# Slice-norm transfers issued by ScalarE and GpSimd in place of SyncE, and a new order of all instructions

## The chip, the cores and the metric

The kernel runs on one core of a Trainium2 chip. Five engines work side by side: TensorE (PE) multiplies matrices, VectorE (DVE) and ScalarE (ACT) do element-wise work, GpSimd (POOL) does small odds and ends, and SyncE (SP) issues the transfers. Each engine takes its own instructions strictly in the order in which the program lists them, and waits on semaphores for the others. An instruction that waits holds everything behind it on its engine. The metric is device time in microseconds; the median of three executions before the change is 2547.61 us (2545.12 to 2547.99).

## What is computed

The input `x` is 32 batches of 512 rows with 256 features, and `adj` is a 512x512 mask. One layer is computed:

```python
x = x + gnn(layernorm(x), adj)     # two graph attention layers
x = x + ffn(layernorm(x))          # attention over slices

# gnn
out = relu(x @ mlp1_w + mlp1_b)                     # 256 -> 512
out = elu(gat(out, None, W_fc, a_fc)) + out         # every row attends to every row
out = relu(out @ mlp2_w + mlp2_b)                   # 512 -> 256
out = relu(elu(gat(out, adj, W_hand, a_hand)) + out)

# ffn: 8 heads of 64, 64 slices
slice_weights = softmax((x_mid @ W_slice + b_slice) / temp)
slice_norm = slice_weights.sum(axis=2)
slice_token = einsum('bhnc,bhng->bhgc', fx_mid, slice_weights) / (slice_norm + 1e-05)
attn = softmax(q @ k.T * SCALE)                     # 64x64 per head, of the tokens
out_x = einsum('bhgc,bhng->bhnc', attn @ v, slice_weights)
return out_x @ W_out + b_out
```

The change concerns how `slice_norm`, a row of 512 sums per batch, travels from the row of a matrix product to the tile that divides the tokens by it.

## The kernel before

The kernel does not issue its operations as it writes them. It builds a list with a recorder: `nc` is a `Recorder`, and each call such as `nc.vector.tensor_tensor(...)` becomes an operation with a batch (`age`) and a stage (`step`). All 32 batches are recorded, batch by batch, as `front` (layer norm, first layer), `middle` (second layer) and `back` (second layer norm and slices). Then `Recorder.order` lays out one order for each engine, and `emit` issues it.

The order comes from list scheduling with a table of costs. `_cost` gives each operation an engine time and a lag; transfers also get a time of moving, during which the modelled transfer queue is taken (`ISSUE`, `BEGIN`, `LAND`, `BEHIND`). `_schedule` then takes, again and again, the operation that can start first, and among those that can start, the one with the lowest key. The keys come from the table `TURNS`, one number per stage, from `PERIOD`, and for the first three and last three batches from the shifts in `HEAD` and `TAIL`. These numbers and the costs decide only which instruction stands where on its engine. On the chip the semaphores decide the times. Up to four batches are in work at once, so that TensorE is given matmuls of one batch while the others do their element-wise work and transfers. In the trace all recorded operations have one line, L289, so groups are told apart by the names of their tiles.

The stages of a batch, with the names that the text below uses:

- `norm1`: layer norm of `xt`. VectorE makes statistics, GpSimd makes `rstd` (two small instructions on 128x4), VectorE makes `xn`.
- `xnT`: the transposed `xn`. In all but the first and last batch, transposes of this size are made in two steps. VectorE flips 32x32 blocks into a stage (`xn_stage`), and SyncE writes the stage to DRAM in four transfers (`scr<-xn_stage`) and reads it back in another order (`xnT<-scr`). The same is done for `u` (to `o1T`), `e` (to `p2T`), `o2` (to `r2`), `w` (to `w_raw`, which ScalarE copies to `wT`) and `xn2` (to `xn2_raw`, which ScalarE copies to `xn2T`).
- `mlp1`, `h`: matmuls of `xnT` with `w1` to `o0T`; then `h` by Strassen's scheme, for which VectorE makes four sums `mix` of blocks of `o0T`.
- `factors`, `p`: a maximum over rows by a transpose of `fm`, a transpose of `sc`, exponentials `acb`, and from them `pT`, the attention matrix of the first layer.
- `pv`, `o1`: 32 matmuls `mm<-h,pT`; the double ELU on VectorE and ScalarE gives `u`, whose transpose is added to `o0T` to make `o1T`.
- `mlp2`, `h2`, `e`, `p2`, `pv2`: the second graph layer, with the matmuls `mm<-o1T,w`, `mm<-wh,o2T` and `mm<-h,p2T`, and a second double ELU, which gives `x1`.
- `norm2`, `w`: the second layer norm, again with `rstd` on GpSimd, gives `xn2` and `xn2T`; the matmuls `mm<-weff,xn2T` and a softmax over each head's 64 slices give `w`, and its flips `w_stage`.
- `sums`, `s1T`: matmuls `mm<-w,xn` sum `xn2` over the rows with the slice weights. The last feature of `xn2` is set to 1, so that the last row of the product holds the norms. ScalarE copies the product to `s1T`.
- `tokens`, `att`, `vo`, `gg`, `out`: small matmuls `mm<-s1T,wfx` make the tokens, VectorE multiplies them by the reciprocal norms (`tok`), a small attention over slices follows (`sc2`, `attT`, `mean`), and 16 matmuls `mm<-gg,wT` give the output, which is added to `x1`.

The norms take this way. Row 127 of `s1T` is one partition with 512 numbers. A transfer spreads it over 128 partitions (`norm`, 128x4); VectorE adds 1e-5 and takes the reciprocal; a second transfer writes it to DRAM (`line`); two more read it back, each to 64 partitions at once (`rn`). Every step waits for the one before. Before the change all four are issued by SyncE, like all other transfers of the batches.

For a batch in the middle SyncE's order before the change runs: `scr<-w_stage` twice, `norm<-s1T`, `scr<-xn_stage` four times, `scr<-w_stage` twice, `xnT<-scr`, `line<-norm`, `w_raw<-scr`, `rn<-line` twice, `scr<-u_stage` four times, `o1T<-scr`, `scr<-xn2_stage` four times, `xn2_raw<-scr`, and then the transfers of `o2`, `out`, `xt`, `e`, `x1` and `p2T`. They belong to different batches.

Of the kernel before, what the change touches and what calls it, by code (L numbers as in the profile page):

```python
# [14 lines left out]
ENGINES = ("tensor", "vector", "scalar", "gpsimd", "sync")  # L15

TURNS = {
    "load": 361.5, "norm1": -64.6, "mlp1": 945.4, "h": 1108, "factors": 1115.3, "p": 1133,
    "pv": 1134.5, "o1": 1135, "mlp2": 1177.7, "h2": 1179.1, "e": 1182.9, "p2": 877, "pv2": 1230.3,
    "norm2": 1235.2, "w": 1273.7, "sums": 1279.8, "s1T": 1239.3, "tokens": 1552, "att": -211,  # L20
    "vo": -118.6, "gg": -952.5, "out": 1227.3,
}
PERIOD, SPARE = 89.08, 0.01

HEAD = (
    (0, -29, 160, 21, 3, -112, -46, -107, 0, -66, -7, -21, -125, -126, 0, 1933, -17, -4, -13, 0,
     9, -230),
    (1280, -6, 24, -107, -16, 42, -95, 0, 52, -257, 0, 10, 10, -15, 6, 922, 199, -1, 61, 0, 14,
     -102),
    (120, 0, 3, 38, 28, 14, 995, 253, 320, -610, 0, 0, 113, -155, 135, -133, -95, 0, -25, 5, -4,  # L30
     -34),
)
TAIL = (
    (279, 0, 0, 0, 0, 17, 0, 0, -104, 0, -939, 31, -14, 0, 1655, 0, 66, 146, 103, 128, 52, 221),
    (-322, 0, -112, 2, -20, 0, -1205, 10, -7, -185, 10, 170, -102, -11, 215, 497, 0, 0, -6, 0,
     76, 63),
    (-107, -134, 0, 190, -47, -204, 0, 86, 13, 5, -3, 0, 4, 11, 273, 574, -226, -28, 78, -10,
     -113, 101),
)


# [4 lines left out]
P = 128  # L46
# [4 lines left out]
class Recorder:  # L51
# [2 lines left out]

    SIGNAL = 0.06
    DRAIN = 0.17
    ISSUE, BEGIN, LAND, BEHIND = 0.45, 2.2, 0.0, 3.6
    SWITCH = 0.17
    KEPT = 1
    AHEAD = 3  # L60
# [66 lines left out]
    def _cost(self, op, out, ins):  # L127


        def words(ap):  # L130
            return ap.size() // ap.ap[0][1]

        n = words(out)
        if op.method == "dma_start":
            side = next(ap for ap in (out, *ins) if ap.space != bass.MemoryType.DRAM)
            kb = out.size() / 256
            if side.ap[0][1] <= P // 4:
                op.moving = 0.3 + max(0.0, 1.08 * (kb / 128 - 1))
            else:
                op.moving = max(1.5 * kb / 512, 4.0 * kb / 1024 - 0.5)  # L140
            return self.ISSUE, 0.0
        if op.engine == "tensor":
            one = max(n / 1200 + 0.002, 0.109)
            if op.mode == (P, P // 2):
                one = max(n / 2400, 0.0275)
            elif op.mode == (P // 2, P // 2):
                one = max(n / 4000, 0.0135)
            return (one if op.method == "transpose" else 2 * one), self.DRAIN
        if op.engine == "scalar":
            pointers = sum(isinstance(op.kwargs.get(k), bass.AP) for k in ("bias", "scale"))  # L150
            return 0.06 + n / 1200 + 0.09 * pointers + 0.19 * ("accum_out" in op.kwargs), 0.12
        if op.engine == "vector":
            n = max([n] + [words(x) for x in ins])
            single = op.method in ("tensor_copy", "tensor_scalar")
            fast = single and all(x.space != bass.MemoryType.PSUM for x in ins)
            if op.method == "reciprocal":
                return 0.05 + n / 145, 0.1
            pointers = sum(words(x) == 1 for x in ins) if n > 1 else 0
            return 0.07 + n / (1920 if fast else 960) + 0.065 * pointers, 0.1
        if n < 16:  # L160
            return (0.1 if op.method == "memset" else 0.3 if op.method == "tensor_scalar" else 1.1), 0.1
        return 0.2 + n / (480 if op.method == "tensor_tensor" else 960), 0.1
# [164 lines left out]
def adj_ffn_kernel(  # L327
# [30 lines left out]
    KD = D // P  # L358
# [5 lines left out]
    NP = INNER // P  # L364
    assert G == C == 64 and HEADS * G == 512 and N == 512 and HID == 512 and D == 256

    nc = Recorder(tc.nc)
# [5 lines left out]
    def ts(i, n=P):  # L373
        return slice(i * n, (i + 1) * n)

    def new(name, shape, bufs=1, tag=None, dtype=F32):
        return sbuf.tile(list(shape), dtype, name=name, tag=tag or name, bufs=bufs)

    def mm_tile(shape):
        return psum.tile(shape, F32, tag="bank", name="mm", bufs=8)  # L380
# [36 lines left out]
    def med(name, shape=(P, 4, 256)):  # L417
        return new(name, shape, bufs=2, tag="med")
# [14 lines left out]
    def load_x(b):  # L433
# [14 lines left out]
        out=ident, in_=ident, compare_op=OP.not_equal, fill=1.0, base=0,  # L448
# [163 lines left out]
    for p in range(NP):  # L612
        pv = mm_tile([P, D])
# [283 lines left out]
    def back(b, x1):  # L897
# [17 lines left out]
        w = new("w", [P, NT, INNER], tag="o0T" if b == B - 1 else None, bufs=1 + (b == B - 1))  # L915
# [34 lines left out]
        s1T = med("s1T", (P, KD, INNER))  # L950
# [14 lines left out]
                )  # L965
        nc.step = "s1T"
        norm = new("norm", [P, NP], bufs=2)
        nc.sync.dma_start(norm, s1T[P - 1 : P, KD - 1, :])
        nc.vector.tensor_scalar(norm, norm, 1e-5, None, op0=OP.add)
        nc.vector.reciprocal(norm, norm)  # L970
        line = dram.tile([NP, 2, G], F32, name="line", tag="line", bufs=2)
        nc.sync.dma_start(line.rearrange("p s (q f) -> (p s q) f", f=NP), norm)
        rn = new("rn", [P, NP, G], tag="mean")
        for s in range(2):
            nc.sync.dma_start(
                rn[ts(s, C)],
                bass.AP(
                    tensor=line.tensor, offset=line.offset + s * G,
                    ap=[[0, C], [2 * G, NP], [1, G]],
                ),  # L980
            )
# [20 lines left out]
        q = new("q", [P, 2, 2, G])  # L1002
# [57 lines left out]
        gg = med("gg")  # L1060
# [33 lines left out]
    for b in range(B):  # L1094
        nc.age = b
        back(b, middle(b, front(b)))
# [57 lines left out]
```

## Time and profile before

| | us |
|---|---|
| median of three executions | 2547.61 |
| lowest and highest | 2545.12, 2547.99 |
| the profiled execution's own time | 2548.94 |
| its span, first to last instruction | 2547.2 |
| VectorE, ScalarE and GpSimd busy | 2041.9, 1095.2, 95.0 |
| transfers, mean share of 16 engines and rate | 49%, 137 GB/s |

The span was taken at a mean granted TensorE clock of 0.995 of full speed. The profile has a page of overviews, and queries for stretches, tiles, waits and an engine's timeline. The slices of the page show the same picture from the first fortieth to the last:

```profile
PE   6999999999999999999999999999999999999998
PEld 5777666666677666666766766666666676667665
DVE  6678778787788887788877888878878878888774
ACT  2544444434435444435344354444443444444442
POOL 0000000000000000000000000000000000000000
```

Each digit is the busy share of a fortieth of the span in tenths. The transfers in question, as the page's list of issues has them, with the issuing queue, count, size and the median time from issue to landing:

```profile
rn<-line SPq DMA_DIRECT2D x64, 64.0 KB, 4.6
...
norm<-s1T SPq DMA_DIRECT2D x32, 2.0 KB, 5.8
line<-norm SPq DMA_DIRECT2D x32, 2.0 KB, 4.3
```

They are small, but each stands in SyncE's queue with everything else.

### The profile page before, as it was taken

The page shows a single profiled execution, that of the slowest core. Times are in us where ns is not written, and L with a number is a line of the kernel's source. Part 1 is how long each engine was busy: PE and PEld are TensorE (multiplying, and loading weights), DVE is VectorE, ACT ScalarE, POOL GpSimd, SP SyncE. Part 2 cuts the span into 40 slices and gives each one's busy share as a digit, 9 for nine tenths or more (in the row PEclk, how much of TensorE's full clock was granted, in tenths as well). Part 3 has the DMA queues.
Part 4 walks back from the last instruction along what each step waited for, and adds up shares of the span by engine and source line. Part 5 has one row for each costly group of instructions (what it writes and reads, how often), then busy time and mean ns, then how long its engine had stood idle before and what let it go on. Part 6 is the DMA issues. An engine that isn't in the chain of part 4 may idle for free.

```text
span 2547.2 us, 34086 instructions
## 1 busy us (share of the span) xinstructions
PE 2493.8 (98%) x11653; PEld 1722.5 (68%) x11653; DVE 2041.9 (80%) x5236; ACT 1095.2 (43%) x2069; POOL 95.0 (4%) x167
## 2 busy tenths in 40 slices
PE   6999999999999999999999999999999999999998
PEld 5777666666677666666766766666666676667665
DVE  6678778787788887788877888878878878888774
ACT  2544444434435444435344354444443444444442
POOL 0000000000000000000000000000000000000000
PEclk8999999999999999999999999999999999999999
DMA  5134455544555544655445554445554455553532
GB/s 161 50 91 111 135 167 154 156 126 119 157 159 159 137 127 124 166 159 151 138 121 143 159 159 135 125 125 168 158 153 133 127 143 161 158 146 106 161 82 63
DMA packets 451139, 348.69 MB, mean 137 GB/s; under 512 B 110228, under 2 KB 375572, under 8 KB 450966
## 3 DMA queue, kind: packets, MB, share of 16 engines
q1 hardware_dynamic: 449382, 345.46, 49.1%
q8 instruction: 93, 1.52, 0.2%
q10 hardware_dynamic: 1584, 1.05, 0.1%
q14 instruction: 80, 0.66, 0.1%
HBM read 186.92 MB, written 159.45 MB: 136 GB/s over the span
## 4 chain that ended last, share of the span: by engine, by line
PE 59%; DVE 20%; DMA 12%; ACT 6%; issue 2%; SPq 1%; POOL 0%; DVEq 0%; ACTq 0%
PE mm L289 57%; DMA scr<-w_stage 4%; DMA w_raw<-scr 3%; DVE e L289 3%; DVE w L289 3%; PE tr L289 2%; DVE rs L289 2%; DVE w_stage L289 2%; DVE e_stage L289 1%; DVE pT L289 1%; ACT acb L289 1%; DMA scr<-xn_stage 1%; DMA xn_raw<-scr 1%; DVE mx L289 1%; DVE x L289 1%
## 5 line engine op out<-in xcount | busy, mean ns | idle before, releaser
L289 PE MATMUL mm<-h,pT 128*128 128x257 f32 (+1 forms) x2048 | 466.3, 380 | 4.0 <-DVE pT L289 4.0
L289 PEld LDWEIGHTS mm<-h,pT 128*128 128x128 f32 x2048 | 387.0, 190 | 107.3 <-issue 50.0
L289 PE MATMUL mm<-weff,xn2T 128*128 128x512 f32 x512 | 255.4, 601 | 5.9 <-ACT xn2T L289 5.7
L289 PE MATMUL mm<-o1T,w 128*128 128x512 f32 x512 | 241.3, 596 | 0.0
L289 PE MATMUL mm<-xnT,w 128*128 128x512 f32 x512 | 234.1, 599 | 7.2 <-DMA xnT<-scr 5.4
L289 PE MATMUL mm<-w,xn 128*128 128x512 f32 x512 | 239.7, 593 | 0.2 <-DVE w L289 0.2
L289 PE MATMUL mm<-gg,wT 128*128 128x256 f32 x1024 | 237.9, 382 | 0.8 <-DVE gg L289 0.8
L289 PEld LDWEIGHTS mm<-gg,wT 128*128 128x128 f32 x1024 | 193.7, 191 | 64.1 <-issue 30.8
L289 PE MATMUL mm<-h,p2T 128*128 128x257 f32 x1024 | 232.5, 380 | 0.7 <-DMA p2T<-scr 0.7
L289 PEld LDWEIGHTS mm<-h,p2T 128*128 128x128 f32 x1024 | 194.0, 190 | 43.1 <-issue 16.4
L289 ACT ACTIVATE w<-w 128x512 f32<-128x512 f32 x128 | 80.6, 630 | 314.8 <-DVE w L289 314.7
L289 ACT ACTIVATE u<-mm,rd 128x256 f32<-128x256 f32 x192 | 89.9, 468 | 220.3 <-DVE rd L289 174.5
L289 DVE TENSOR_TENSOR h<-mm,h 128x257 f32<-128x257 f32 x320 | 131.0, 411 | 57.5 <-PE mm L289 57.2
L289 ACT ACTIVATE m<-m 128x512 f32<-128x512 f32 x192 | 120.4, 628 | 125.9 <-DVE m L289 125.8
L289 ACT COPY q<-mm 128x256 f32<-128x256 f32 x32 | 11.9, 371 | 370.3 <-PE mm L289 370.3
L289 PEld LDWEIGHTS mm<-xnT,w 128*128 128x128 f32 x512 | 96.4, 191 | 108.1 <-issue 95.0
L289 DVE SCALAR_TENSOR_TENSOR u<-m,u 128x512 f32<-128x512 f32 x192 | 130.8, 682 | 34.9 <-ACT m L289 34.0
L289 PEld LDWEIGHTS mm<-o1T,w 128*128 128x128 f32 x512 | 94.4, 189 | 78.0 <-issue 58.7
L289 PEld LDWEIGHTS mm<-w,xn 128*128 128x128 f32 x512 | 93.1, 189 | 76.6 <-issue 59.8
L289 ACT COPY h<-mm 128x257 f32<-128x257 f32 (+1 forms) x256 | 92.7, 371 | 111.2 <-PE mm L289 110.8
L289 ACT ACTIVATE m<-m,neg 128x512 f32<-128x512 f32 x192 | 138.0, 720 | 3.4
L289 PE MATMUL mm<-wfc,mix 128*128 128x257 f32 x512 | 137.6, 385 | 0.0
(155 smaller groups left out, 4150.6 us busy)
## 6 DMA issues: line engine op xcount, KB each, us to landing
scr<-xn_stage SPq DMA_DIRECT2D x240, 128.0 KB, 2.5
scr<-u_stage SPq DMA_DIRECT2D x120, 256.0 KB, 4.6
o1T<-scr SPq DMA_DIRECT2D x30, 1024.0 KB, 5.3
scr<-e_stage SPq DMA_DIRECT2D x120, 256.0 KB, 4.3
p2T<-scr SPq DMA_DIRECT2D x30, 1024.0 KB, 8.0
scr<-w_stage SPq DMA_DIRECT2D x120, 256.0 KB, 4.5
w_raw<-scr SPq DMA_DIRECT2D x30, 1024.0 KB, 8.0
x<-in_x_dram SPq DMA_DIRECT2D x32, 512.0 KB, 5.6
```

The costliest lines, as they stand in the source:

```text
L289: getattr(getattr(self.nc, op.engine), op.method)(*op.args, **op.kwargs)
```

## The change

Two things are changed. The transfer of the norms out of `s1T` is issued by ScalarE, and the three that follow by GpSimd. And the order of all instructions on all engines is laid out anew: the tables `TURNS`, `HEAD` and `TAIL` and the number `PERIOD` have new values, and so have the costs by which the scheduler places transfers and ScalarE's activations that do not read PSUM.

```diff
 TURNS = {
-    "load": 361.5, "norm1": -64.6, "mlp1": 945.4, "h": 1108, "factors": 1115.3, "p": 1133,
-    "pv": 1134.5, "o1": 1135, "mlp2": 1177.7, "h2": 1179.1, "e": 1182.9, "p2": 877, "pv2": 1230.3,
+    "load": 2173.3, "norm1": 40.8, "mlp1": 574.6, "h": 861.5, "factors": 920.1, "p": -252.9,
+    "pv": 755.1, "o1": 830.2, "mlp2": 861.5, "h2": 241.9, "e": 691.5, "p2": 4.6, "pv2": 1066.9,
...
 }
-PERIOD, SPARE = 89.08, 0.01
+PERIOD, SPARE = 117.08, 0.01
...
-    ISSUE, BEGIN, LAND, BEHIND = 0.45, 2.2, 0.0, 3.6
+    ISSUE, BEGIN, LAND, BEHIND = 0.45, 1.2, 0.75, 2.7
...
-            if side.ap[0][1] <= P // 4:
-                op.moving = 0.3 + max(0.0, 1.08 * (kb / 128 - 1))
+            if op.engine != "sync" and op.age >= 0:
+                return (0.1, 2.6) if op.engine == "scalar" else (1.0, 2.6)
+            if kb <= 64:
+                op.moving = 0.61
+            elif side.ap[0][1] <= P // 4:
+                op.moving = 1.12 * kb / 256
+            elif out.space == bass.MemoryType.DRAM:
+                op.moving = 1.1 * kb / 512
             else:
-                op.moving = max(1.5 * kb / 512, 4.0 * kb / 1024 - 0.5)
+                op.moving = 2.0 * kb / 512
...
-            return 0.06 + n / 1200 + 0.09 * pointers + 0.19 * ("accum_out" in op.kwargs), 0.12
+            near = op.method == "activation" and ins[0].space != bass.MemoryType.PSUM
+            return 0.06 + n / 1200 + 0.04 * near + 0.09 * pointers + 0.19 * ("accum_out" in op.kwargs), 0.12
...
-        nc.sync.dma_start(norm, s1T[P - 1 : P, KD - 1, :])
+        nc.scalar.dma_start(norm, s1T[P - 1 : P, KD - 1, :])
         nc.vector.tensor_scalar(norm, norm, 1e-5, None, op0=OP.add)
         nc.vector.reciprocal(norm, norm)
         line = dram.tile([NP, 2, G], F32, name="line", tag="line", bufs=2)
-        nc.sync.dma_start(line.rearrange("p s (q f) -> (p s q) f", f=NP), norm)
+        nc.gpsimd.dma_start(line.rearrange("p s (q f) -> (p s q) f", f=NP), norm)
         rn = new("rn", [P, NP, G], tag="mean")
         for s in range(2):
-            nc.sync.dma_start(
+            nc.gpsimd.dma_start(
```

The other entries of the tables change in the same way and are left out. For a batch in the middle SyncE's order after the change, as the built program has it, runs: `scr<-xn_stage` four times, `scr<-w_stage` four times, `xnT<-scr`, `scr<-u_stage` four times, `w_raw<-scr`, `o1T<-scr`, `scr<-xn2_stage` four times, `xn2_raw<-scr`, `scr<-o2_stage` four times, `r2<-scr`, `out`, `xt`, `x1`, `scr<-e_stage` four times, `p2T<-scr`. On GpSimd `line<-norm` and `rn<-line` stand ahead of the two small instructions for `rstd` of the next batch's second layer norm.

## The prediction

> **What bounds the kernel now.** I read the page's busy times first, then busy time by stretch, then TensorE's waits in the middle, then the chain of waits.
>
> ```profile
> PE 2493.8 (98%) x11653; PEld 1722.5 (68%) x11653; DVE 2041.9 (80%) x5236; ACT 1095.2 (43%) x2069; POOL 95.0 (4%) x167
> ```
> ```profile
> 0.00:80.00 80.00, 60.20 (x225) 42.91 (x226) 55.87 (x168) 22.73 (x40) 5.91 (x16) 0.89 0.52 147
> 80.00:2400.00 2320.00, 2298.74 (x10716) 1589.73 (x10715) 1887.48 (x4826) 1013.43 (x1922) 86.41 (x145) 1.00 0.51 140
> 2400.00:2547.20 147.20, 134.83 (x715) 89.84 (x713) 98.58 (x244) 59.03 (x107) 2.70 (x6) 0.98 0.30 82
> ```
> TensorE (PE) is the bound: second column is the stretch's length, third PE's busy time. It idles 19.8 us in the first 80, 21.3 in the middle 2320 and 12.4 in the last 147. No matmul is added or removed, so the change can only move these 53 us and the small drains counted as busy. What PE waits for in the middle:
> ```profile
> PE mm L289 <- DMA xnT<-scr: 5.4, 5, 2.7
> PE tr L289 <- DVE sc L289: 5.4, 24, 0.2
> PE mm L289 <- ACT xn2T L289: 5.2, 5, 1.6
> ```
> Two gathers that come late in some batches, and one short VectorE (DVE) wait in nearly every batch. The same group of matmuls stands in each batch of the chain of waits; its start gives the period:
> ```profile
> 453.12 1.75 PE mm L289 x6
> ...
> 765.56 1.75 PE mm L289 x6
> ...
> 842.25 1.75 PE mm L289 x6
> ...
> 1307.83 1.75 PE mm L289 x6
> ...
> 1389.17 1.75 PE mm L289 x6
> ...
> 2240.74 1.75 PE mm L289 x6
> ```
> First to last of these is 1787.62 us in 23 periods: 77.72 each. The best is 76.69, the worst 81.34. How the worst comes about is in SyncE's timeline, with PE's wait at its end:
> ```profile
> 1344.33 2.77 SPq L289 DMA_DIRECT2D scr<-xn_stage  x3
> 1347.13 1.02 SPq L289 DMA_DIRECT2D scr<-w_stage  x2
> 1350.70 0.38 SPq L289 DMA_DIRECT2D xnT<-scr  x1
> 1351.18 0.41 SPq L289 DMA_DIRECT2D line<-norm  x1
> 1351.98 0.36 SPq L289 DMA_DIRECT2D w_raw<-scr  x1
> 1356.66 1.25 SPq L289 DMA_DIRECT2D rn<-line  x2
> ```
> ```profile
> 1356.61 2.39 PE L289 MATMUL mm<-xnT,w 128*128 128x512 f32 x3 [2.72 <-DMA xnT<-scr]
> ```
> SyncE issues in order. The norm's transfer stands ahead of these rows and waits for ScalarE's (ACT) copy of s1T; xn_stage, half of w_stage and the gather of xnT stand behind it. rn then holds the queue from 1352.3 to 1356.7 until line has landed. In all SyncE waits 81.9 us for line and 40.9 for s1T.
>
> [...] on SP the norm takes 5.8 us (median) to land amid other transfers, and 2.0 in the quiet end. [...] No POOL transfer is in this trace.
>
> **The change, part by part.** Estimates below add row durations along the instruction order of the built changed kernel; back-to-back cadences are a 257-column matmul 0.433 us, a 512-column one 0.858, ACT 512 wide 0.61, DVE 512 wide 0.6.
>
> *Issue.* SP loses four issues per batch (0.54+0.41+2x0.61 = 2.2 us) and the two waits. ACT gains one issue, about 0.5 us at 43% load, behind its first s1T copy. POOL gains three, [...] it is 4% busy. The second layer norm's rstd (0.23+1.04 us) now stands behind rn on POOL: the norm lands about 3 us after the last w,xn matmul, POOL is free about 7 later, and rstd is due about 15 after that matmul. Hidden, with 5 us to spare. rn's reader, tok, came 39 us after that matmul; in the new order PE has 34.8 us of work there, against a chain of 12 to 15. Hidden.
>
> *xnT.* New SP order: four xn_stage, four w_stage, xnT. Nothing waits for s1T. From the last softmax matmul (weff) to xnT's first reader PE has 24.7 us of work. The softmax of the last row block and its flip end 14 us after it in DVE's order, then w_stage 4.5 and xnT 3.8 to land: about 22. The wait goes.
>
> *xn2T.* From the last p2T matmul to its reader PE has 22.9 us of work now and 27.1 after; in one period the path took 24 (971.7 to 995.8). The wait goes.
>
> *sc.* PE covers 1.72 us from the transpose of fm to that of sc in both. Before, two reduce/subtract pairs of the slice attention (4x0.2) stand on DVE between them; after, only tok's rest, f2m 0.2, a flip 0.63 and ex/sc 0.25. sc is ready about 1.8 after the token matmuls, PE arrives at 1.83. That takes away 9.1 us over 26 waits by the page's rows: 0.35 a batch.
>
> *New tight places.* The first h,pT matmul moves from 18.4 us of PE work behind sc to 4.7; its path (acb 0.69, exp 1.06, ACT pT 0.73, DVE pT 0.75, ordered behind the small softmax) adds to 4.5. attT, behind four pT copies and an h2 copy on ACT, is ready at 8.05 against PE's 8.02. DVE's norm instruction now stands 2.9 us after the last w,xn matmul; the quiet chain (copy 0.6, 2.5 to DVE, the issue starting 0.2 before that matmul ends) needs 2.3 to 2.5. Behind it wait u_stage, the second ELU, mix and the o1T additions, with about 1 us to spare before PE. I allow 0.5 us a batch for these, from nothing to 1.3.
>
> Middle: 77.72 - (76.69 - 0.35 + 0.5) = 0.88 us for each of 28 batches: 24.6 us gained.
>
> *Start.* Two waits are long:
> ```profile
> 27.00 3.79 PE L289 MATMUL mm<-mixed,mix 128*128 128x257 f32 x8 [4.77 <-DVE mix L289]
> ...
> 52.38 1.23 PE L289 MATMUL mm<-h,pT 128*128 128x257 f32 x2 [4.04 <-DVE pT L289]
> ```
> After, DVE does the needed mix before the adjacency mask (eight instructions, 2.9 us), and of the second batch's norm and flips (4x(0.33+0.08+0.32+0.33) = 4.2 us) only three statistics stay ahead of pT: 3.2 less. Adding durations, the first h,pT starts near 44 to 48 where it started at 52.4, as PE then waits for wx and for free banks instead. I take 6 us gained, range 2 to 8.
>
> *End.* From the last w,xn matmul to tok PE has 11.1, 10.2 and 8.2 us of work in the last three batches, 8.0, 8.0 and 8.9 after. SP's chain took 12.0, 12.6 and 7.7. The new chain, estimated: copy 0.6, norm 2.5, DVE 0.4, line 1+2, rn 1+1+2: 10.5. Short by 0.9+2.4+0 = 3.3 before, 2.5+2.5+1.6 = 6.6 after: 3.3 lost.
>
> Sum: 24.6 + 6 - 3.3 = 27.3 us off the profiled execution's 2548.94, which stands 1.3 over the median: 2521.6 there, 2520.3 by the median. I say 2522.
>
> **The rivals.** *B, nothing gained.* The norm on ACT's ring lands as late as on SP (DVE 6.1 us after the issue). DVE waits about 3 us more in each batch, 0.9 of it beyond its room before the o1T additions: 25 us in 28 batches, which eats the middle's gain: 2522 + 25 = 2547. For it: the engines move 140 GB/s just then. [...]
>
> *C, slower.* [...] short by 25.5 in the last three batches (22 more than now) and, with 14.5, 12.8 and 13.2 of cover, by 10 in the first three. [...] Sum -30.6+22+10+14 = +15: 2563. [...] Against: POOL's arithmetic runs beside a busy DVE now, mostly at 1.04 us.
>
> *D, more gained.* No new wait: 28x(1.03+0.35) = 38.6, start 8, end 0: 2501.
>
> **How the numbers follow.** Forecast 0.52 (its own range 2508 to 2538), B 0.15, C 0.22, D 0.11. Below about 5 us (0.2%) a change of this kernel cannot be told from none. Faster: forecast 0.50, D 0.11, B 0.03: 0.64. Same: 0.13, mostly B. Slower: 0.23, C and a little of B. The range leaves out most of C and the lower half of D: 2503 to 2553.
>
> **What would show it.** Right: no PE waits for xnT or xn2T, the period of the repeated group near 76.8 with little spread, h,pT first near 46, norm to DVE near 2.5 us. Wrong: DVE waiting for norm in each batch (B); [...] PE waiting for tok in the first and last batches (C); PE waiting for attT or pT by over 0.5 us a batch, which the forecast did not price.

## The result, and the profile after

The changed kernel takes 2558.45 us (median of 19 runs, 2550.61 to 2570.40) where the kernel before takes 2547.87 on the same chip (19 runs, 2540.97 to 2554.85). The ratio is 1.0045, with a 95% interval of 1.0031 to 1.0058. A second set of runs on another chip gave 1.0066 (1.0048 to 1.0085). The forecast was 2522, a gain; by the medians the kernel became slower, by 11 us on the first chip and by 18 on the second.

The profiled execution after has a span of 2566.2 and an own time of 2567.99, which is 9.5 above the median. So single places are read from it here, and sizes from a second pair of profiles further down. The page's busy times, and the same three stretches as before (second column the length, third PE's busy time, third from the end the granted clock):

```profile
PE 2502.0 (97%) x11653; PEld 1735.8 (68%) x11653; DVE 2050.9 (80%) x5236; ACT 1123.5 (44%) x2069; POOL 157.1 (6%) x263
```
```profile
0.00:80.00 80.00, 63.57 (x236) 44.34 (x237) 55.81 (x168) 23.64 (x41) 5.90 (x16) 0.94 0.48 143
80.00:2400.00 2320.00, 2294.00 (x10643) 1596.04 (x10642) 1890.34 (x4814) 1038.76 (x1913) 142.97 (x232) 1.00 0.51 140
2400.00:2566.20 166.20, 144.42 (x778) 95.47 (x776) 104.74 (x256) 61.12 (x116) 8.27 (x15) 0.92 0.28 79
```

PE idles 16.4 us in the first 80 (19.8 before), 26.0 in the middle (21.3) and 21.8 in the last stretch (12.4). The start gained a little; the other two lost. The middle stretch holds batches 0 to 4 too, in which the pipeline still fills; a table further down takes them apart. PE's waits in the middle stretch (the one line of all recorded operations has another number in each kernel, L297 here):

```profile
PE mm L297 <- DVE o1T L297: 7.5, 12, 1.4
PE mm L297 <- DVE tok L297: 4.4, 2, 3.4
PE mm L297 <- DVE mix L297: 3.6, 1, 3.6
PE mm L297 <- DMA p2T<-scr: 3.1, 3, 1.6
...
PE tr L297 <- DVE sc L297: 0.4, 2, 0.3
```

The waits for xnT and xn2T are gone, and that for sc fell from 5.4 us to 0.4. In their place stand o1T in 12 batches, and tok and mix, which come late because a norm came late: mix stands behind tok on VectorE, and in batch 4 VectorE stands still for 6.8 us ahead of tok until rn has landed. The period of the repeated group of matmuls, from the chain of waits:

```profile
850.53 1.73 PE mm L297 x6
...
927.25 1.73 PE mm L297 x6
...
1003.97 1.73 PE mm L297 x6
```

76.72 us twice. The best period before was 76.69, so the new order's best period is no shorter. Nor is it reached more often: from batch 5 to 26, counted at the last `mm<-w,xn` matmul of each batch, 5 of 21 periods are within 0.01 us of the best in both profiles. What fell is the mean of the 21, from 77.60 to 77.30. The norm's own transfers, from the list of issues, with the median time to landing in the last column:

```profile
rn<-line POOLq DMA_DIRECT2D x64, 64.0 KB, 6.0
...
norm<-s1T ACTq DMA_DIRECT2D x32, 2.0 KB, 3.4
line<-norm POOLq DMA_DIRECT2D x32, 2.0 KB, 6.0
```

The norm lands sooner (3.4 against 5.8), but line and rn land later (6.0 each against 4.3 and 4.6). What that does where there is little cover is seen in batch 29. First the timeline of POOL, then of VectorE, then of PE, then the granted clock by short stretches:

```profile
2453.49 0.64 POOL L297 DMA_DIRECT2D line<-norm  x1 [0.78 <-DVE norm L297]
2460.14 1.23 POOL L297 DMA_DIRECT2D rn<-line  x2 [6.01 <-DMA line<-norm]
```
```profile
2465.14 0.42 DVE L297 TENSOR_TENSOR tok<-mm,rn 128x256 f32<-128x256 f32 x1 [9.27 <-DMA rn<-line]
```
```profile
2454.78 3.60 PE L297 MATMUL mm<-o1T,w 128*128 128x512 f32 x8
2465.61 1.22 PE L297 MATMUL mm<-tok,wqk 128*128 128x256 f32 x2 [7.23 <-DVE tok L297]
```
```profile
2450.00:2458.00 8.00, 8.00 (x49) 3.78 (x47) 4.25 (x17) 0.59 (x2) 2.02 (x4) 1.00 0.66 203
2458.00:2466.00 8.00, 0.77 (x2) 0.39 (x2) 0.42 (x1) 2.17 (x4) 1.23 (x2) 0.76 0.51 123
2466.00:2470.00 4.00, 2.16 (x20) 0.93 (x19) 1.07 (x4) 1.72 (x5) 0.00 (x0) 0.50 0.00 0
2470.00:2474.00 4.00, 3.88 (x6) 1.71 (x7) 1.80 (x5) 1.54 (x4) 0.00 (x0) 0.50 0.00 0
2474.00:2478.00 4.00, 4.00 (x30) 2.94 (x29) 2.80 (x5) 1.92 (x5) 0.00 (x0) 0.77 0.46 94
```

POOL writes line at 2453.5 and can issue rn only at 2460.1. VectorE stands idle for 9.27 us, because tok is next in its order. PE waits 7.23 us, until 2465.6. Within the wait the granted clock, the third column from the end, goes from 1.00 to 0.50, and it is back at 1.00 near 2476 (0.76 and 0.77 are means of stretches in which it changes). So PE runs at half the clock for some 10 us behind the wait, and its matmuls take longer there: four of 128x512 take 3.78 us at 2470.1 (`mm<-weff,xn2T`), where four take 1.88 at 2450.1 (`mm<-o1T,w`). What the half clock adds to the time of the kernel is not shown.

Last, SyncE. The forecast said that it loses its waits. The list of its own waits has this line:

```profile
SPq L297 <- DMA norm<-s1T: 39.3, 21, 2.6
```

SyncE no longer issues the norm's transfer, and still waits 39.3 us for it to land.

### The profile page after: what moved, and what is told of

The parts are those of the page before. It is cut to its first block, busy times and chain, and to the rows that moved or that the text cites. A ratio compares the mean times of both kernels' runs of the same rounds, so it can differ in the third digit from the quotient of the medians.

```text
span 2566.2 us, 34111 instructions
## 1 busy us (share of the span) xinstructions
PE 2502.0 (97%) x11653; PEld 1735.8 (68%) x11653; DVE 2050.9 (80%) x5236; ACT 1123.5 (44%) x2069; POOL 157.1 (6%) x263
## 3 DMA queue, kind: packets, MB, share of 16 engines
q1 hardware_dynamic: 422758, 341.13, 48.6%
## 4 chain that ended last, share of the span: by engine, by line
PE 71%; DMA 13%; DVE 10%; ACT 3%; issue 2%; SPq 1%; POOL 0%; DVEq 0%; ACTq 0%; POOLq 0%
PE mm L297 68%; DMA w_raw<-scr 4%; PE tr L297 3%; DMA o1T<-scr 2%; DMA line<-norm 2%; DMA rn<-line 1%; DMA norm<-s1T 1%; DMA scr<-u_stage 1%; DVE e L297 1%; ACT m L297 1%; DVE w L297 1%; DVE u L297 1%; DVE xn L297 1%; SPq L297 1%; DVE m L297 1%
## 5 line engine op out<-in xcount | busy, mean ns | idle before, releaser
L297 PE MATMUL mm<-h,pT 128*128 128x257 f32 (+1 forms) x2048 | 498.6, 383 | 4.7 <-DVE pT L297 3.3
L297 PEld LDWEIGHTS mm<-h,pT 128*128 128x128 f32 x2048 | 381.7, 190 | 160.3 <-issue 83.0
L297 DVE TENSOR_TENSOR h<-mm,h 128x257 f32<-128x257 f32 x320 | 131.5, 420 | 160.8 <-PE mm L297 140.8
L297 PE MATMUL mm<-weff,xn2T 128*128 128x512 f32 x512 | 253.3, 602 | 1.7 <-ACT xn2T L297 1.7
L297 PE MATMUL mm<-w,xn 128*128 128x512 f32 x512 | 251.9, 593 | 0.8 <-DVE w L297 0.7
L297 PE MATMUL mm<-o1T,w 128*128 128x512 f32 x512 | 229.3, 596 | 7.7 <-DVE o1T L297 7.5
L297 PE MATMUL mm<-h,p2T 128*128 128x257 f32 x1024 | 230.6, 382 | 3.2 <-DMA p2T<-scr 3.1
L297 PE MATMUL mm<-gg,wT 128*128 128x256 f32 x1024 | 231.4, 382 | 0.8 <-DVE gg L297 0.8
L297 PE MATMUL mm<-xnT,w 128*128 128x512 f32 x512 | 229.8, 597 | 0.5 <-ACT xnT L297 0.5
L297 PEld LDWEIGHTS mm<-h,p2T 128*128 128x128 f32 x1024 | 194.9, 191 | 45.3 <-issue 12.1
L297 PEld LDWEIGHTS mm<-gg,wT 128*128 128x128 f32 x1024 | 195.6, 192 | 43.1 <-DVE gg L297 9.0
L297 ACT ACTIVATE u<-mm,rd 128x256 f32<-128x256 f32 x192 | 90.7, 474 | 250.2 <-DVE rd L297 184.8
L297 ACT ACTIVATE m<-m 128x512 f32<-128x512 f32 x192 | 120.9, 630 | 174.1 <-DVE m L297 171.1
L297 ACT ACTIVATE w<-w 128x512 f32<-128x512 f32 x128 | 80.4, 629 | 218.4 <-DVE w L297 218.3
L297 PEld LDWEIGHTS mm<-o1T,w 128*128 128x128 f32 x512 | 95.1, 190 | 118.5 <-issue 85.5
L297 PEld LDWEIGHTS mm<-xnT,w 128*128 128x128 f32 x512 | 97.0, 191 | 107.5 <-issue 99.0
L297 ACT COPY xn2T<-xn_raw 128x512 f32<-128x512 f32 x60 | 34.3, 615 | 296.7 <-DMA xn_raw<-scr 296.7
L297 DVE SCALAR_TENSOR_TENSOR u<-m,u 128x512 f32<-128x512 f32 x192 | 131.0, 682 | 40.7 <-ACT m L297 38.6
L297 ACT ACTIVATE m<-m,neg 128x512 f32<-128x512 f32 x192 | 138.3, 720 | 5.1
L297 PEld LDWEIGHTS mm<-weff,xn2T 128*128 128x128 f32 x512 | 91.7, 193 | 56.0 <-issue 42.2
L297 PEld LDWEIGHTS mm<-w,xn 128*128 128x128 f32 x512 | 96.0, 189 | 43.3 <-issue 31.3
L297 PE MATMUL mm<-mixed,mix 128*128 128x257 f32 x512 | 119.5, 384 | 4.5 <-DVE mix L297 4.5
```

The source lines that it names most:

```text
L297: getattr(getattr(self.nc, op.engine), op.method)(*op.args, **op.kwargs)
```

## The experiments

Three theories after the result. *L*: line and rn by GpSimd land late, and batches at both ends have too little TensorE work to cover it. *O*: the new order is what costs. *S*: GpSimd, issuing these transfers, holds VectorE. Later came *G*: GpSimd's transfers make SyncE's large ones land late. *A*: ScalarE's norm does that. *P*: SyncE's waits kept the large transfers apart. *T*: a tie by shared semaphores, explained below.

All edits but those named are in `emit`, where the engine of an operation is looked up, so that the order of every other instruction stays:

```diff
-            getattr(getattr(self.nc, op.engine), op.method)(*op.args, **op.kwargs)
+            engine = op.engine
+            if op.step == "s1T" and op.method == "dma_start":
+                engine = ...
+            getattr(getattr(self.nc, engine), op.method)(*op.args, **op.kwargs)
```

### Order and issue apart

With `"scalar"` for the norm and `"gpsimd"` for the rest in the old order:

> The order and costs of before; only the norm's transfer is issued by ScalarE and line and rn by GpSimd, at the places where SyncE issued them. Theory L (the new issue is good in the middle, but line and rn by GpSimd land so late that tok holds VectorE where a batch has little TensorE work between its last w,xn matmul and tok): in this order only the last three batches are short of cover, so the middle loses its waits for xnT and the end loses about 4 us: ratio to before 0.992 to 0.998. Theory O (the new order is what costs, the issue is good everywhere): 0.987 to 0.993. Theory S [...]: 1.002 to 1.010.

Measured: 1.0174 (1.0148 to 1.0200). Every theory missed. Half of the change, in the order before, costs 44 us.

With `"sync"` for all in the new order:

> The order of after, with all four norm transfers issued by SyncE at the places the layout gave them. Theory L: line and rn land about 1.5 us sooner each in the short batches at both ends, which gives back some 10 us there, but SyncE again waits for line in each batch and o1T, behind rn, comes later: about 0.5 to 1 us a batch, so 1.002 to 1.010 in all. Theory O: the same order with a slower issue, 1.008 to 1.015. Theory S: below after's 1.0045, near 1.000 or less, since GpSimd issues nothing.

Measured: 1.0039 (1.0025 to 1.0053). This lies in L's range, below O's. The other half alone costs nearly what the whole does. From the last `mm<-w,xn` matmul of batch 5 to that of batch 26 this run took 1613.3 us, with 19 of its 21 periods at 76.71 or 76.72. S falls as the main cause: without any transfer by GpSimd most of the loss is there.

SyncE for line and rn in the ten batches at the ends only, `if engine == "gpsimd" and not 5 <= op.age <= 26: engine = "sync"`:

> After, but line and rn are issued by SyncE in batches 0 to 4 and 27 to 31, where TensorE has only 8 to 14 us of work between the last w,xn matmul and tok; the norm stays with ScalarE and the 22 batches between keep GpSimd. Theory L: 8 to 15 us less than after, ratio to before 0.998 to 1.001. Theory O: no change to after within 3 us, 1.003 to 1.006. Theory S: a third of the batches lose their GpSimd issue, 1.002 to 1.004.

Measured: 1.0033 (1.0020 to 1.0047), 3 to 8 us less than after: L's direction, less than its size. By the ratio this is as much O's result (1.003 to 1.006) as L's; the next run tells the two apart. By SyncE line takes 4.9 us to land there and rn 2.7, and tok still comes 12.5 to 18.1 us after the last w,xn matmul in batches 0 to 4.

The chain left out at both ends:

```diff
+            if op.step == "s1T" and not 5 <= op.age <= 26:
+                if op.args[0].tensor.name.startswith("rn"):
+                    self.nc.gpsimd.memset(op.args[0], 1.0)
+                continue
```

> After, but batches 0 to 4 and 27 to 31 leave out the norm's transfer, the two VectorE instructions on it, line and rn; rn is filled with ones by one GpSimd instruction at the place of each rn transfer, so tok waits for nothing there. All other work is done. This is the most that a faster norm chain at the two ends can give. Theory L: 20 to 30 us less than after, ratio to before 0.992 to 0.997. Theory O: at most 5 us less than after, 1.002 to 1.005. Theory S: a third of the loss goes, 1.001 to 1.003.

Measured: 0.9992 (0.9979 to 1.0004). What the norms cost at the ends is 0.5% to 0.7% of the time, 13 to 19 us, which is all of the loss. O's and S's ranges are missed. L has the place, but its 20 to 30 us was too large, and GpSimd is the smaller part of it: with SyncE issuing line and rn there only 3 to 8 us came back. By either engine the chain is longer than what covers it.

Why the ends cannot cover the chain is seen in the times of tok, in us from the last w,xn matmul of the batch (before and after from the second pair of profiles below):

| batch | 1 | 2 | 3 | 4 | 27 | 28 | 29 | 30 | 31 |
|---|---|---|---|---|---|---|---|---|---|
| before | 25.1 | 19.7 | 38.7 | 39.3 | 39.5 | 20.8 | 12.0 | 12.4 | 7.9 |
| after | 17.2 | 12.8 | 16.9 | 20.1 | 17.2 | 14.9 | 12.6 | 11.7 | 8.8 |
| new order, no chain at the ends | 12.1 | 10.8 | 13.5 | 13.4 | 14.0 | 14.9 | 5.2 | 10.9 | 8.8 |

The new order is ready for tok far sooner than the old one in batches 1 to 4, and the chain does not come sooner with it. Near the end, batches 27 and 29 wait for their norms; in 28 and 31 tok comes no sooner without them.

### Which of the issuing engines

The four other combinations:

> The order of after, the norm by ScalarE, line and rn by SyncE. Measured so far from the last w,xn matmul of batch 5 to that of batch 26: 1629.5 us before, 1623.3 after, 1613.3 with everything on SyncE in the new order. Theory G (line and rn by GpSimd make the large transfers on SyncE's queue land later, in every batch, and land late themselves where cover is short): this stretch stays near 1613 to 1615, the start and the end are those of the run with only the ends by SyncE (batch 5 at 568, end 359 after batch 26), so about 2541 in all, 0.998 to 1.001. Theory A (the norm by ScalarE, beside SyncE's transfers, is what delays them): the stretch is near after's 1623, 1.001 to 1.005.

> The order of after, the norm by SyncE, line and rn by GpSimd. Theory G: from batch 5 to batch 26 near after's 1623, u_stage's landing near 5.8 us again where it is 4.1 with everything on SyncE, tok late in the first and last batches as in after: 1.003 to 1.007. Theory A: near 1613 in the middle, 0.999 to 1.003.

> The order of before, the norm by ScalarE, line and rn by SyncE. With norm, line and rn all moved this order ran 1669.7 us from batch 5 to batch 26 where before ran 1629.5. Theory G: near before's 1629 or up to 15 us below, as SyncE no longer waits for s1T: 0.994 to 1.002. Theory A: most of the 40 us is here: 1.010 to 1.017. Theory P (SyncE's waits for s1T and line keep the large transfers apart, and any of them taken away packs them): a part of it, as one wait of the two is gone: 1.003 to 1.010.

> The order of before, the norm by SyncE, line and rn by GpSimd. Theory G: most of the loss is here, xnT's landing near 5.8 us against 3.8 before, 1.010 to 1.017. Theory A: 0.994 to 1.002. Theory P: the wait for line, the longer of the two (81.9 us against 40.9), is gone: 1.006 to 1.013, with u_stage issued 1 to 2 us sooner behind xnT.

| order | norm by | line, rn by | ratio | 95% interval |
|---|---|---|---|---|
| old | ScalarE | SyncE | 1.0074 | 1.0051 to 1.0097 |
| old | SyncE | GpSimd | 1.0037 | 1.0026 to 1.0047 |
| old | ScalarE | GpSimd | 1.0174 | 1.0148 to 1.0200 |
| new | SyncE | SyncE | 1.0039 | 1.0025 to 1.0053 |
| new | ScalarE | SyncE | 1.0028 | 1.0019 to 1.0036 |
| new | SyncE | GpSimd | 1.0096 | 1.0073 to 1.0119 |
| new | ScalarE | GpSimd (after) | 1.0045 | 1.0031 to 1.0058 |

In the new order line and rn are better on SyncE: by 0.6% with the norm by SyncE, by 0.2% with it by ScalarE (0.4% with the 1.0066 of the second set), G's side. In the old order each move alone costs, and both together cost more than their sum. The first of the four runs has G's middle (1614.4 us) with a total in A's range, the second lies above both ranges, the third in P's, the fourth in none: none of G, A and P as stated. The norm, line and rn land in 2.7, 3.5 and 6.7 us (medians) with all by SyncE in the new order, and in 3.4, 6.0 and 6.0 after.

Then the pair again on one chip, for the stages, with two tests beside it:

> The kernel before once more, for its stages on the chip of the three runs beside it; on another chip it ran 355.2 us from the last w,xn matmul of batch 0 to that of batch 5, 1629.5 on to batch 26 and 351.7 from there to the end. Every theory expects ratio 1; if the new order is worth 16 us in the middle, as the runs on different chips suggest, the stretch from 5 to 26 is again near 1629, and if part of that was the chip, 1618 to 1624.

> The changed kernel once more, on the chip of the runs beside it. Ratio 1.003 to 1.006; from batch 0 to 5 about 400 to 406 us, from 5 to 26 about 1620, from 26 to the end about 360, with a wait for tok of some 7 us in batch 29 and TensorE's granted clock at half for some 15 us after it.

Measured: spans 2540.2 and 2557.4 (the middle of before lies between its two expectations, after is just over its range), medians 2541.93 (one run) and 2556.28 (ratio 1.0066). The stages, from the ends of the last `mm<-w,xn` matmuls in the timeline of PE. The first two rows are estimates of TensorE's own work up to these points, cadences added along the instruction order as in the prediction, since the two orders take up the batches differently:

| us | to batch 0 | 0 to 5 | 5 to 26 | 26 to the end |
|---|---|---|---|---|
| work, old order | 179.7 | 344.4 | 1583.9 | 324.4 |
| work, new order | 150.0 | 381.0 | 1583.9 | 317.5 |
| before, again | 207.7 | 355.3 | 1626.0 | 351.3 |
| after, again | 176.6 | 403.3 | 1619.2 | 358.3 |
| after less before, beyond the work | -1.4 | +11.4 | -6.8 | +13.9 |
| new order, no chain at the ends | 174.0 | 389.2 | 1617.4 | 356.2 |
| new order, no chain at all | 173.7 | 389.1 | 1612.1 | 350.6 |

The runs are from three chips, on which the kernel before ran at 2538.6, 2539.7 and 2535.7 us (medians, in the order of the rows). For example, 176.6 - 207.7 is -31.1, of which 150.0 - 179.7 = -29.7 is work. The last row is a run told below. The middle gained 6.8 us, and the five batches in which the pipeline fills and the last five lost 25.3.

Twelve matmuls that PE can do while it waits in batch 29, `for i in range(12): matmul(op.args[0], wqk, weff[:, 0, :256])` ahead of the matmul of tok:

> After, with twelve extra matmuls of 256 columns (5.2 us) ahead of the tok,wqk matmul of batch 29, into the bank that it overwrites; the result is the same. They stand in the 7 us for which TensorE waits for tok there. Theory K (what a late norm costs at the end is the wait and, as much again, the half clock that TensorE is granted after it): the clock stays at 1.00 after the wait and the run is 3 to 6 us shorter than after, ratio lower by 0.0012 to 0.0024. If the wait's length is all: no change, or up to 1 us longer.

Measured: 1.0066 (1.0045 to 1.0087), as after. The filling itself ended too soon. PE still waited 2.2 us for tok behind it and 1.5 us for xn2T later, and the clock went down all the same, though no single wait there is longer than these, as the stretches 2454 to 2462 of this run show:

```profile
2454.00:2458.00 4.00, 2.04 (x21) 1.03 (x20) 1.63 (x6) 2.72 (x7) 0.00 (x0) 0.74 0.00 0
2458.00:2462.00 4.00, 4.00 (x9) 2.03 (x8) 2.24 (x5) 0.91 (x2) 0.00 (x0) 0.50 0.00 0
```

So nothing was gained; what the half clock costs by itself stays open.

The run with all by SyncE, and GpSimd issuing line and rn once more, to tiles that nothing reads:

> The new order with all four norm transfers by SyncE, as in the earlier run (1.0039; 1613.3 us from batch 5 to 26, u_stage landing in 4.1 us), and beside them GpSimd issues the same line and rn transfers once more, to tiles that nothing reads, so that GpSimd's queue is that of after but no result waits for it, only rstd stands behind it. Theory G (transfers issued by GpSimd make SyncE's land later): u_stage lands in 5.3 to 5.8 us, 1618 to 1623 us from batch 5 to 26, ratio 1.006 to 1.010. Theory W (only who waits for the norms matters): as the earlier run, 1.002 to 1.005.

Measured: 1.0115 (1.0095 to 1.0134), 1627.0 us from batch 5 to 26. Transfers that nobody waits for cost 0.76%, over G's range; W falls. Not as G said, through u_stage: that landed in 4.3 us. w_raw's landing went from 8.4 to 9.5 us and the first o1T matmul came 0.6 us later (21.6 us after the last w,xn matmul against 21.0, medians). PE's waits for o1T in the middle stretch, first with all by SyncE, then with GpSimd's extra transfers:

```profile
PE mm L300 <- DVE o1T L300: 2.4, 3, 0.9
```
```profile
PE mm L300 <- DVE o1T L300: 11.1, 16, 1.8
```

The extra transfers also double the traffic of the chain. Whether it is GpSimd's way of issuing or these bytes is not told apart. That GpSimd holds VectorE is not it: VectorE is busy for 2050.8 us in this run and for 2049.0 with all by SyncE.

### Why the new issue costs so much in the old order

Where the 44 us of the first run went: SyncE's waits, then PE's, in that run.

```profile
SPq L292 <- DMA norm<-s1T: 47.5, 25, 2.9
```
```profile
PE mm L292 <- DMA xnT<-scr: 41.8, 22, 3.2
```

One batch of it, ScalarE's and SyncE's timelines, and PE's wait:

```profile
1130.90 0.48 ACTq L292 DMA_DIRECT2D norm<-s1T  x1
```
```profile
1132.75 3.42 SPq L292 DMA_DIRECT2D scr<-xn_stage  x4
1136.21 1.76 SPq L292 DMA_DIRECT2D scr<-w_stage  x2
1138.33 0.62 SPq L292 DMA_DIRECT2D xnT<-scr  x1
```
```profile
1145.64 4.94 PE L292 MATMUL mm<-xnT,w 128*128 128x512 f32 x7 [2.98 <-DMA xnT<-scr]
```

The norm is issued at 1130.9. SyncE takes 3.42 us for four xn_stage; 2.04 in a batch of before. It stops ahead of the fourth of them, which is issued 5.9 us after the last w,xn matmul (median of batches 5 to 26; 4.1 before), when the norm has landed. The trace tells why: in 26 batches the next transfer to signal the norm's semaphore is that fourth xn_stage. The trace of after shows the same of another transfer. SyncE's and ScalarE's transfers signal the same eight semaphores there, in 26 batches a u_stage is the next to signal the norm's, and all 21 of SyncE's waits for the norm (39.3 us) stand ahead of that u_stage. Moved to another engine's queue, the norm is still tied to SyncE. GpSimd's 96 transfers signal eight other semaphores. Hence the next runs, all four transfers by GpSimd, in the old order and in the new:

> The order of before, all four norm transfers by GpSimd. With the norm by ScalarE and line and rn by GpSimd this order ran at 1.0174, SyncE waited 47.5 us for the norm and xnT's gather came late in 22 batches (41.8 us). Theory T (the tie by the shared completion semaphores makes SyncE's last xn_stage wait for ScalarE's norm): the tie is gone, SyncE waits for no norm, PE's wait for xnT falls below 10 us, ratio 1.001 to 1.006. Theory G (GpSimd's transfers as such make SyncE's land late): one more of them, 1.017 or more.

Measured: 1.0061 (1.0046 to 1.0076). SyncE's list of waits has no norm in it, the fourth xn_stage is issued at 4.0 us, and PE waits for xnT 11.0 us where it waited 41.8 (just over T's 10). One more transfer by GpSimd, and 29 us less. T stands, just over its range; G as the cause of the 44 us falls. But the tie alone does not cost 44 us either: it is there in the old order with line and rn by SyncE (1.0074), where SyncE waits 45.2 us for the norm in its profile, and PE only 10.1 for xnT. It takes both, the tie and GpSimd's line and rn. That the landing of xnT in this run is 4.1 us (median) against 5.8 fits.

> The order of after, all four norm transfers by GpSimd. Theory T: SyncE issues the first u_stage 0.3 to 0.4 us sooner after the last w,xn matmul than in after (4.2 us there), the middle from batch 5 to 26 is near 1615 us against 1619 to 1623; the norm lands 2 us later, which the short batches at the ends pay: 1.004 to 1.008 in all. Theory G: 1620 us or more in the middle and 1.008 to 1.012 in all.

Measured: 1.0151 (1.0135 to 1.0167), 1625.9 us in the middle, the first u_stage at 4.7 us, later and not sooner. T's expectation missed; G has the middle, but not the total. In this order the tie costs little: with line and rn by SyncE the middle takes 1613.3 us with the norm by SyncE and 1614.4 with it by ScalarE. What binds is that VectorE's instruction on the norm stands ahead of the flips of u. VectorE's waits for the norm, first after, again, then in this run:

```profile
DVE norm L297 <- DMA norm<-s1T: 11.4, 22, 1.5
```
```profile
DVE norm L300 <- DMA norm<-s1T: 29.7, 29, 4.0
```

A norm that VectorE gets later moves u_stage, o1T and PE behind it. In this run PE waits for o1T 9.4 us in 12 batches of the stretch from 600 to 2180 (3.2 in 4 after, again). The end lost as much as the middle: 366.6 us from batch 26 on, 358.3 after, again.

### What the order is worth without norms

The chain left out of all batches, by the edit above without its limit on the batch:

> The order of after without any norm transfer: the norm's transfer, the two VectorE instructions on it, line and rn are left out in all batches, rn is filled with ones by GpSimd. This is what the new order is worth when the norms cost nothing. If the norms' transfers are what holds the middle, 1611 to 1613 us from batch 5 to 26 (21 periods of 76.72), 0.995 to 0.998; if the order's own tight places hold it, 1617 to 1620 as in the run without the chain at the ends, 0.998 to 1.000.

Measured: 0.9968 (0.9956 to 0.9980), and 1612.1 us in the middle: 20 of 21 periods are 76.71 or 76.72. So the transfers of the norms, not the order's other tight places, hold the middle of after. And the new order without norms is 8 us faster than the old one with them. The old order without norms was not run, so how much of the 8 us is the order is open. From this run to that without the chain at the ends the ratio rises by 0.0024, 6 us for the chain in the 22 middle batches; from there to after by 0.0053 to 0.0074, 13 to 19 us for the ten at the ends.

Spreading the norms at the ends by small matmuls in place of transfers:

```diff
+                for p in range(4):
+                    self.nc.tensor.matmul(
+                        cols[:, p : p + 1], sums[:, p * P : p * P + P], self.ident[:, P - 1 : P],
+                        start=True, stop=True,
+                    )
...
+            self.nc.tensor.matmul(rows[half], self.ones[half], rn[half], start=True, stop=True)
+        self.nc.scalar.copy(rn, rows)
```

> The order of after, in batches 5 to 26 the norm by ScalarE and line and rn by SyncE (that ran at 1.0028). In batches 0 to 4 and 27 to 31 no transfer: four matmuls of one column turn the row of norms into columns, VectorE adds 1e-5, takes reciprocals of 128x4 and multiplies them into a 64x64 unit matrix, two matmuls by ones spread them over the partitions, ScalarE copies them to rn. The result is the same. The chain is then about 4 us instead of 13 to 17 and stays within the cover of 8 to 14 us: ends as in the run without the chain there, 0.9985 to 0.9999 less 3 us for the middle by SyncE: 0.996 to 0.999. If the added VectorE and TensorE work (1 to 1.5 us a batch) is late itself, 1.000 to 1.002.

Measured: 1.0070 (1.0057 to 1.0082). The middle was as expected (1614.5), the ends were not (399.3 and 363.2). The second pair of matmuls was put 40 TensorE instructions behind the first, some 12 us later in batch 1, and tok came 10.4 to 17.7 us after the last w,xn matmul: no sooner than by transfers. The placing was at fault, so this says nothing of the idea.

The order laid out again with larger costs for the norms' transfers:

```diff
-                return (0.1, 2.6) if op.engine == "scalar" else (1.0, 2.6)
+                return (0.1, 3.4) if op.engine == "scalar" else (0.65, 4.5)
```

> After, laid out with 3.4 us for the norm's transfer and 0.65 and 4.5 us for each of GpSimd's in place of 2.6 and 1.0 and 2.6; the engines that issue are those of after. Theory L (the loss at the ends is the norm chain outlasting the cover that the layout left): 390 to 396 us from batch 0 to 5 where after has 403 to 406, 354 to 358 from batch 26 to the end where after has 358 to 361, ratio 0.999 to 1.002. If the cover is only taken from other paths there (the last batch's xn2T has 5.5 us of TensorE work ahead of it where after has 8.0): within 3 us of after, 1.003 to 1.006.

> The order of the run beside it, the norm by ScalarE, line and rn by SyncE in all batches (in after's order that issue ran at 1.0028, with 1614 us from batch 5 to 26). Theory L: 3 to 6 us less than the run beside it, ratio 0.997 to 1.000. Otherwise 1.002 to 1.004.

Measured: 1.0079 (1.0065 to 1.0093) and 1.0054 (1.0040 to 1.0069); 406.3 and 363.5 us at the ends in the first. Theory L's remedy failed, and the other expectation came closer; only the 6 us between the two runs are near what L had. PE waits for tok 0.9 us only, but in the last 364 us of the first run it waits for other things:

```profile
PE mm L297 <- ACT xn2T L297: 8.7, 1, 8.7
PE tr L297 <- DVE xn L297: 5.9, 1, 5.9
```

Work put ahead of tok was taken from ahead of xn2T and xn. Of the wait for xn, 2.9 us are the norm again: VectorE waits for the last batch's norm ahead of it. No order tried here had enough work for all of these places at the end. No run that does the whole computation beat the kernel before; the best was the new order with the norm by ScalarE and line and rn by SyncE, 1.0028.

## Why the prediction was wrong

The step that failed is the reckoning of the norms' chain at the ends. Outside the middle the sum held it against the cover of the last three batches alone, and counted there only TensorE's wait for tok. But in batches 1 to 4 tok waited for the chain until 13 to 20 us after the last w,xn matmul. The stretch from batch 0 to batch 5 lost 11.4 us, which stood in no term; without any chain it gains 2.8 (389.1 less 355.3 and 36.6 of work). At the end the loss was 13.9 in place of 3.3. Line and rn took 6.0 us each to land (medians; 3.5 and 6.7 by SyncE in the new order), where 2 each were reckoned. Without the chain at both ends the loss is gone (0.9992). Beside this the middle's gain was sized too large.

In numbers, the forecast of 27.3 us gained and the second pair's 17.1 us lost are 44.4 apart. *Start* up to batch 0 gained 1.4 in place of 6: 4.6. The next five batches lost 11.4. *Middle* from batch 5 to 26 gained 6.8 where 21 times 0.88 is 18.5: 11.7. The other seven of its 28 batches lie in the stretches at the ends and were to gain 6.2 more. *End* lost 13.9 in place of 3.3: 10.6.

*Issue* failed too, at less cost. "SP loses four issues per batch ... and the two waits": it lost the waits for line and for ScalarE's copy, and got a wait for the norm's landing, 39.3 us in 21 batches, that neither diff nor timeline of before shows. The semaphores that the transfers signal, in the traces of the changed kernels, do. In the new order the wait falls ahead of u_stage and costs little; in the old one, together with GpSimd's line and rn, it made up 29 of the 44 us. POOL's issue was sized at 1.0 us, in the chain at the ends too: a guess, since no trace of before has a transfer by POOL. It took 0.64.

*xnT*, *xn2T* and *sc* were right: all three waits went. They were worth less than priced. From batch 5 to 26 the period fell from 77.43 to 77.10 on one chip (1626.0/21 and 1619.2/21): 0.33, not 0.88. The 77.72 of the sum was too high a start: it took in one more period at each end (79.4 and 78.8), and its execution ran at 77.60 from batch 5 to 26. And the 0.35 for sc came back: the best period is 76.72, not 76.34, with no norm at all too. *New tight places* had warned of pT: in such a period the second weight load of the h,pT matmuls starts 0.05 us after VectorE has written its pT. Its allowance of 0.5, from nothing to 1.3, has to read 77.10 - 76.34 = 0.76.

*Start*: the first h,pT matmul came at 48.2 and 48.6 us, just past "44 to 48", but the second profile of before has it at 49.4, not 52.4. The step stopped there. The five batches behind it, whose cover had been listed only for rival C, and only for three of them, have the larger loss.

*End* had the waits for tok nearly right. Forecast: 6.6 us in the last three batches; measured after, again: 4.9 in batch 29, none in batch 30 and 0.3 in batch 31. But the end lost 13.9 in place of 3.3. Of that 7.7 go with the whole chain left out (13.9 - 6.2, the last row of the table less before, beyond the work): more than the waits for tok. VectorE's standstill and the half clock are likely parts of the rest, not shown one by one. The other 6.2 belong to the order of the end itself, which the forecast took as equal; how they come about stays open.

Rival C had the place right, the first and the last batches, and nearly the time, 2563, but by luck. It supposed that GpSimd's transfers take far longer to issue beside a busy VectorE, and that issuing them takes time from VectorE, which is the 14 in its sum. Both were the author's guesses, and neither is seen: POOL's issues take 0.62 to 0.65 us (means of rn and line) with VectorE 80% busy, and VectorE is busy for 2050.8 us with GpSimd's extra transfers and for 2049.0 without any. The time is lost in landing, which the last section takes apart. Rival B fell: the norm lands in 3.4 us by ScalarE. But it is the new place in the order that did it, not the engine that issues it: by SyncE it lands in 2.7 us in the new order, and by ScalarE in 4.9 in the old one, against 5.8 by SyncE. D's premise, no new wait, was met only where no norm was transferred at all, and even then the gain was 8 us, not 46.

## What to carry to other kernels

Moving a transfer to another engine's queue frees the first queue only if nothing else ties them (here SyncE still waited 39.3 us for a norm that ScalarE issued): look in the built program for the semaphore that it will signal, and which transfer waits for that one next. Price a chain of small dependent transfers by its measured landing times under load, for every batch and not for the period alone: where the pipeline fills and drains the cover was 8 to 14 us here, where it was 35 in the middle. And take the floor of an order (all suspected waits left out) before adding up what removed waits are worth: here it was 8 us, where the forecast said 27.

## What was not expected of the hardware

How long such a small transfer takes to land was not given here by its size or its engine. line has 2 KB. By GpSimd it took 1.7 to 8.4 us in the one profile of after, with a median of 6.0; by SyncE at nearly the same place in the new order 3.5; and in the old order 4.1 by GpSimd and 4.3 by SyncE. Of the 6 us hardly any is moving: in batches 5 to 26 of after 3.0 pass before its first packet, 0.6 from there to its last, and 2.5 until the completion is seen (medians). What the 2.5 us are spent on, no run shows.

The time before the first packet goes with the other transfers and not with VectorE. For rn by GpSimd, over all twelve traces that have it, the medians are (number of transfers in brackets):

| issue to first packet of rn, us | DMA engines under 30% busy with others | over 70% |
|---|---|---|
| VectorE under 30% busy | 1.35 (16) | 2.40 (9) |
| VectorE over 80% busy | 1.37 (27) | 2.85 (274) |

A busy VectorE adds 0.02 us where the other transfers are few and 0.45 where they are many; the other transfers add over 1 us. So GpSimd waiting for VectorE, on which rival C rested, is not what makes these transfers late. And transfers that nothing waits for were not free: 96 more of them by GpSimd, 4.3 MB beside 349, cost 19 us by the two ratios (1.0115 and 1.0039).
